# Local attention of a fused four-layer network: smaller pieces, one issue order read from a table, integer steps as two-operand instructions

## Chip, cores, metric

One NeuronCore of a Trainium2 chip runs the whole network as one launch. The metric is device time in microseconds (us) from start to end of the launch; lower is better. The core has five engines with queues of their own: PE (TensorE, matrix products; weight loads are listed as PEld), DVE (VectorE), ACT (ScalarE), POOL (GpSimd) and SP (which issues DMAs here). Each runs its instructions in the order of its queue and waits on semaphores for the others.

## What is computed

Four layers, each `x = x + attention(norm(x)) * silu(ffn(norm(x)))`, on x of 16 x 256 x 128 in fp32. The change lies in the feed-forward branch of the fourth layer, which is itself a small transformer of depth 2, and at its start in the end of the third layer (a mixture of experts, whose rows are gathered and weighted). Cut to what matters:

```python
def _layer(x, wqkv, qs, ksc, wo, lg, lb, w1, b1, w2, b2):     # DEPTH = 2 times
    h = shift_token(x)                        # second half of the columns moved by one token
    q, k, v = split(h @ wqkv)                 # 8 heads of 64
    q = l2norm(q) * qs ; k = l2norm(k) * ksc
    q, k = rotary_xpos(q, k)
    o = local_attention(q, k, v)              # windows of 64, each sees itself and the one before
    x = x + o @ wo
    h = shift_token(x)
    h = layernorm(h) * lg + lb
    a, g = split(h @ w1 + b1)
    return x + (a * gelu(g)) @ w2 + b2

# end of the third layer:
x = x + s * silu(sum over the 2 chosen experts of gate * (relu(x @ W1[e] + b1) @ W2[e] + b2[e]))
xn = layernorm(x)                             # input of the fourth layer
```

## The kernel before

`layer3` calls `local_attention` twice, with `gated_mlp` after each. I call the two calls the first and the second pass. Each works on 16 batches (b) of 256 tokens, which are two tiles (t) of 128 tokens on the partitions. For every batch it does, by the names of its inner functions (before, after in brackets where a letter is used):

- `begin`, `begun` (B, h; L1773, L1778, L1779, in the first pass also L1781): transpose the input tile on PE, copy it shifted into hT on ACT.
- `times` (T, V; L1785): one 128 x 512 projection on PE; j = 0 is q, 1 is k, 2 is v; twice each for the two tiles.
- `squares` (q; L1795): squares of q or k on ACT. `turned` (c, r; L1803 to L1812): their sums by head and the rotation, four instructions on DVE, and the sum `rot += sn` on POOL.
- `values` (v; L1818, L1821): copy of v on ACT, and a DMA from SP's queue that moves a half to other partitions.
- `lengths` (L, k; L1825, then `rsqrt` L1728 to L1738, and L1831): the inverse root of the lengths by an integer guess and three Newton steps, 13 instructions of 32 columns on DVE; then k is scaled on POOL, twice.
- `across` (X, x; L1838, L1841): q or k turned to have its columns on the partitions, PE then ACT.
- `scores` (S, m; L1849, L1858, L1867, L1869): for one half u of the heads, mask and 32 small products on PE into two PSUM banks (pool `ps`), then the negated maxima on DVE, times the lengths.
- `powers` (e; L1881): four exponentials of 128 x 128 on ACT with their sums; `shares` (d, p; L1894, L1895): reciprocal on DVE, scaling on POOL.
- `keys_first` (K, y; L1903, L1907): probabilities turned on PE, copied on ACT. `weigh` (W, o; L1916, L1926): 12 products with v on PE into the one bank of pool `po`, copied on ACT.
- `finish`, `finished` (F, A; L1932, L1941): output projection, and the sum into x on DVE.

The issue order is written out in a loop over i: the scores of batch i stand beside the projections of batch i+2, the turning of batch i+1 and the last half of batch i-1. `pin` ties every instruction to the one before it on its engine, so this order is each engine's order. PSUM has eight banks here: three rotate under the name `pm` (pt, pj, pr and pw, in order of allocation), two `ps`, two `pt`, one `po`. In SBUF, `sq` and `sn` have two buffers each, `rot` three, `p` and `pT` five.

In the first pass, `end(n)` from the third layer is called seven times ahead of the loop and twice in each round: it gathers two expert rows for tile n (L1508, an indirect DMA of POOL's queue, into three `got` buffers per name), weighs those of tile n-1 on DVE (L1518), and in a cycle of four takes one chunk of four tiles through the gated sum (Silu on ACT at L207, two products on DVE at L208, L209), the statistics (L896, L897, and a power on POOL, L158, L159) and the normalising (L904), which gives the next input tiles.

The function that makes the integer guess, before the change:

```python
nc.vector.tensor_scalar(guess, x.bitcast(I32), 1, None, ALU.logical_shift_right)              # L1728
nc.vector.tensor_scalar(guess, guess, -1.0, float(0x5F3759DF), ALU.mult, ALU.add)             # L1729
```

Of the kernel before, what the change touches and what calls it, by code (L numbers as in the profile page):

```python
# [72 lines left out]

class Net:
    def __init__(self, tc, ctx, a):
        self.tc, self.nc, self.a, self.ctx = tc, tc.nc, a, ctx
        nc = self.nc
        self.keep = ctx.enter_context(tc.tile_pool(name="keep", bufs=1))
        self.x = self.keep.tile([P, NT, D], F32, name="x")
        self.xn = self.keep.tile([P, NT, D], F32, name="xn")  # L80
        self.xnT = self.keep.tile([P, NT * P], F32, name="xnT")
        self.s = self.keep.tile([P, NT, D], F32, name="s")
        self.ident = self.const("ident")
        self.ones = self.keep.tile([P, P], F32, name="ones")
        nc.vector.memset(self.ones, 1.0)
        self.again = self.keep.tile([P, NT], F32, name="again")
        self.desc, self.before = self.const("desc"), self.const("before")
        self.mhalf = self.keep.tile([P, 32], F32, name="mhalf")
        nc.vector.memset(self.mhalf, -0.5)
# [741 lines left out]
    def layer2(self, ydram, consts, fin):  # L831
# [58 lines left out]
        at = {}  # L890

        def stats(c):
            mv = fin.tile([P, 4, 2], F32, name="ln_mv")
            for j in range(4):
                st = fin.tile([P, 6], F32, name="ln_st")
                nc.vector.bn_stats(st, self.x[:, 4 * c + j, :])  # L896
                nc.vector.bn_aggr(mv[:, j, :], st)  # L897
            at[c] = mv, self.rstd(fin, mv[:, :, 1], 4, EPS, "ln_r")

        def normed(c):  # L900
            mv, r = at.pop(c)
            for j in range(4):
                t = 4 * c + j
                nc.vector.tensor_scalar(  # L904
                    self.xn[:, t, :], self.x[:, t, :], mv[:, j, 0:1], r[:, j : j + 1], ALU.subtract, ALU.mult
                )

        def end(pool, n):


            if 0 <= n < NT:
                experts["bring"](pool, n)
            if 0 <= n - 1 < NT:
                experts["weigh"](n - 1)
            c, r = divmod(n - 5, 4)
            if 0 <= c < NT // 4 and r == 0:
                self.gated_add(fin, 4 * c, chunk(f, c), 4)
            if 0 <= c < NT // 4 and r == 1:
                stats(c)
            if 0 <= c < NT // 4 and r == 2:  # L920
                normed(c)

        return end
# [723 lines left out]
    def layer3(self, end, out):  # L1647
# [6 lines left out]
        with ExitStack() as ctx:  # L1654
            gp = ctx.enter_context(right("a3_g"))
            dram = ctx.enter_context(tc.tile_pool(name="a3_d", bufs=1, space=DRAM))
            for l in range(2):
                with right(f"f3_m{l}") as cp:
                    d = self.local_weights(cp, l)
                    mlp = self.mlp_weights(cp, l)  # L1660
                    if l == 0:
                        with tc.tile_pool(name="l2_g", bufs=3) as got:
                            self.local_attention(X, d, lambda n: end(got, n))
# [60 lines left out]
    def rsqrt(self, pool, x, n, name):  # L1724
# [3 lines left out]
        nc.vector.tensor_scalar(guess, x.bitcast(I32), 1, None, ALU.logical_shift_right)  # L1728
        nc.vector.tensor_scalar(guess, guess, -1.0, float(0x5F3759DF), ALU.mult, ALU.add)  # L1729
# [12 lines left out]
    def local_attention(self, X, d, end=None):  # L1742

# [7 lines left out]
        with ExitStack() as ctx:  # L1751
# [18 lines left out]
            def begin(b):  # L1770
# [4 lines left out]
            def begun(b):  # L1775
# [7 lines left out]
            def times(b, t, j):  # L1783
# [9 lines left out]
            def squares(b, t, j):  # L1793
# [3 lines left out]
            def turned(b, t, j):  # L1797
                if t == 0 and j == 0:
                    rows[b]["ss"] = vp.tile([P, 2, 2, 8], F32, name="ss")
                    rows[b]["rot"] = rp.tile([P, 2, 2, 512], F32, name="rot")  # L1800
                pj, sq = rows[b].pop(("pj", t, j)), rows[b].pop(("sq", t, j))
                rot = rows[b]["rot"][:, t, j, :]
                nc.vector.tensor_reduce(rows[b]["ss"][:, t, j, :], heads(sq), AX.X, ALU.add)  # L1803
                nc.vector.tensor_mul(heads(rot), heads(pj), wide(d["cos"][:, t, j, :]))
                sn = pool.tile([P, 512], F32, name="sn")
# [6 lines left out]
                nc.gpsimd.tensor_add(rot, rot, sn)  # L1812

            def values(b, t):
                if t == 0:
                    rows[b]["v"] = vv.tile([P, 3, 512], F32, name="v")
                v = rows[b]["v"]
# [5 lines left out]
            def lengths(b):  # L1823
                ss = rows[b]["ss"].rearrange("p t j h -> p (t j h)")
                nc.vector.tensor_scalar_max(ss, ss, 1e-24)  # L1825
                r = self.rsqrt(vp, ss, 32, "rl")
                rows[b]["r"] = r.rearrange("p (t j h) -> p t j h", t=2, j=2)
                for t in range(2):
                    k = heads(rows[b]["rot"][:, t, 1, :])
                    n = rows[b]["r"][:, t, 1, :].rearrange("p (h o) -> p h o", o=1)  # L1830
                    nc.gpsimd.tensor_mul(k, k, n.to_broadcast([P, 8, 64]))  # L1831

            def across(b, j):
                out = pool.tile([P, 4, S], F32, name="qk"[j] + "T")
                for t in range(2):
                    pr = psm.tile([P, 4, P], F32, name="pm")
                    for c in range(4):
                        nc.tensor.transpose(  # L1838
                            pr[:, c, :], rows[b]["rot"][:, t, j, c * P : (c + 1) * P], self.ident
                        )  # L1840
                    nc.scalar.copy(out[:, :, t * P : (t + 1) * P], pr)  # L1841
                rows[b]["qk"[j]] = out

            def scores(b, u):

                qT, kT, r = rows[b]["q"], rows[b]["k"], rows[b]["r"]
                ps = [psc.tile([P, 2, 2, P], F32, name="ps") for _ in range(2)]
# [4 lines left out]
                for c in range(2):  # L1852
                    for w, keys in enumerate(((0, 0), (64, 128))):
                        for half in range(2):
                            q0 = P * w + 64 * half
                            for i in range(2):
# [7 lines left out]
                                )  # L1864
                for i in range(2):
                    nm = vp.tile([P, 2, 2], F32, name="nm")
                    nc.vector.tensor_reduce(nm, ps[i], AX.X, ALU.max, negate=True)  # L1867
                    h = 4 * u + i
                    nc.vector.tensor_mul(  # L1869
                        nm, nm, r[:, :, 0, h : h + 3 : 2].rearrange("p w c -> p c w")  # L1870
                    )
                    rows[b]["ps", u, i] = ps[i], nm

            def powers(b, u, i):
                ps, nm = rows[b].pop(("ps", u, i))
# [3 lines left out]
                for c in range(2):  # L1879
                    for w in range(2):  # L1880
                        nc.scalar.activation(  # L1881
                            p[:, c, w, :],
                            ps[:, c, w, :],
                            AF.Exp,
                            scale=rows[b]["r"][:, w, 0, h + 2 * c : h + 2 * c + 1],
                            bias=nm[:, c, w : w + 1],
# [5 lines left out]
            def shares(b, u, i):  # L1892
                p, den = rows[b]["p", u, i], rows[b].pop(("den", u, i))
                nc.vector.reciprocal(den, den)  # L1894
# [4 lines left out]
            def keys_first(b, c):  # L1899
                pt = pst.tile([P, 2, 2, P], F32, name="pt")  # L1900
                for i in range(2):
                    for w in range(2):
                        nc.tensor.transpose(  # L1903
                            pt[:, i, w, :], rows[b]["p", c // 2, i][:, c % 2, w, :], self.ident
                        )
                rows[b]["pT", c] = pT = pp.tile([P, 2, 2, P], F32, name="pT")
                nc.scalar.copy(pT, pt)  # L1907

            def weigh(b, c):

                po = pso.tile([P, S], F32, name="po")
# [12 lines left out]
                if c == 0:  # L1924
                    rows[b]["o"] = pool.tile([P, 4, S], F32, name="oT")
                nc.scalar.copy(rows[b]["o"][:, c, :], po)  # L1926

            def finish(b):
                rows[b]["pw"] = pw = psm.tile([P, 2, D], F32, name="pm")
                for t in range(2):  # L1930
                    for c in range(4):
                        nc.tensor.matmul(  # L1932
                            pw[:, t, :],
                            rows[b]["o"][:, c, t * P : (t + 1) * P],
# [5 lines left out]
            def finished(b):  # L1940
# [3 lines left out]
            def run(f, b, *args):  # L1944
                if 0 <= b < B:
                    f(b, *args)

            mark = len(nc.cur_bb.bb.instructions)
            if end is not None:
                for n in range(7):  # L1950
                    end(n)
            for i in range(-3, B + 1):
                run(scores, i, 0)
                run(times, i + 2, 0, 0)
                run(squares, i + 2, 0, 0)
                run(powers, i, 0, 0)
                run(times, i + 2, 0, 1)
                run(squares, i + 2, 0, 1)
                run(turned, i + 2, 0, 0)
                run(keys_first, i - 1, 2)  # L1960
                run(powers, i, 0, 1)
                run(shares, i, 0, 0)
                run(turned, i + 2, 0, 1)
                run(keys_first, i - 1, 3)
                run(shares, i, 0, 1)
                run(across, i + 1, 0)
                run(weigh, i - 1, 2)
                run(times, i + 2, 0, 2)
                run(values, i + 2, 0)
                run(weigh, i - 1, 3)  # L1970
                if end is not None:
                    end(2 * i + 13)
                run(scores, i, 1)
                run(times, i + 2, 1, 0)
                run(squares, i + 2, 1, 0)
                run(powers, i, 1, 0)
                run(times, i + 2, 1, 1)
                run(turned, i + 2, 1, 0)
                run(squares, i + 2, 1, 1)
                run(finish, i - 1)  # L1980
                run(shares, i, 1, 0)
                run(finished, i - 1)
                run(powers, i, 1, 1)
                run(turned, i + 2, 1, 1)
                run(keys_first, i, 0)
# [116 lines left out]
```

## Time and profile before

| what | value |
|---|---|
| three runs (us) | 2974.58, 2992.75, 2987.36; median 2987.36 |
| the profiled execution | 2966.91, its span 2965.2 |
| busy in the span: PE, DVE, ACT, POOL | 2391.3 (81%), 1984.8 (67%), 1559.5 (53%), 1360.3 (46%) |
| first pass | 1548 to 1955 us of the span |
| second pass | 2087 to 2454 us |
| first pass: busy PE, DVE, ACT, POOL (1548 to 1965) | 329.4, 315.3, 285.8, 237.9 of 417 |
| second pass: the same (2084 to 2455) | 295.1, 254.9, 258.3, 179.0 of 371 |

The two passes are about a quarter of the span, and in neither is an engine busy throughout. A span is read best by stages: the shares of the whole mix stages with different limits. A line of the order of time gives start, length, engine, line, operation, what it writes and reads, how many instructions are merged in it, and in brackets how long the engine sat idle before it and what ended that.

### The profile page before, as it was taken

To read this page: it belongs to the slowest core of one execution; us is meant where nothing else is said; L and a number is where in the kernel's file an instruction comes from. 1 tells how busy PE (TensorE), PEld (TensorE's weight loads), DVE (VectorE), ACT (ScalarE), POOL (GpSimd) and SP (SyncE) were. 2 spreads that over 40 slices of the span, in tenths; PEclk is the share of its full clock that TensorE was granted. 3 is DMA by queue.
4 is the path that set the end of the run, shared out by engine and by line. 5 is a ranking of instruction groups with operands and counts; after the bars stand their busy time and mean duration, and the time that the engine had idled before them with its cause. 6 is when DMAs were issued, how large, how long until landed. Compare 5 with 4: busy or idle time off the path is not lost.

```text
span 2965.2 us, 47535 instructions
## 1 busy us (share of the span) xinstructions
PE 2391.3 (81%) x17543; PEld 1561.1 (53%) x17543; DVE 1984.8 (67%) x3841; ACT 1559.5 (53%) x3490; POOL 1360.3 (46%) x1084
## 2 busy tenths in 40 slices
PE   5999983669856589998967787868788878789988
PEld 3666662556532355555544555555355555555555
DVE  4666523335479788888869888624677744488885
ACT  1555561213344466666636777721577763456564
POOL 2000002113236666666666665432455533299896
PEclk8999986779967899999987999978999999899898
DMA  2111002000013455555540000000100000111110
GB/s 64 27 26 30 12 4 98 4 15 13 16 59 123 145 172 188 180 175 187 187 141 26 22 25 17 12 1 0 45 14 14 14 8 4 39 38 45 31 48 8
DMA packets 136915, 168.88 MB, mean 57 GB/s; under 512 B 20850, under 2 KB 100988, under 8 KB 136684
## 3 DMA queue, kind: packets, MB, share of 16 engines
q1 hardware_dynamic: 128108, 147.75, 17.1%
q0 software_dynamic: 6496, 17.05, 1.7%
q8 instruction: 139, 2.28, 0.3%
q10 hardware_dynamic: 2080, 1.05, 0.1%
q14 instruction: 92, 0.75, 0.1%
HBM read 127.62 MB, written 29.79 MB: 53 GB/s over the span
## 4 chain that ended last, share of the span: by engine, by line
PE 24%; DVE 15%; ACT 14%; POOL 8%; issue 3%; DMA 3%; SPq 1%; POOLq 0%; DVEq 0%; ACTq 0%
ACT p L1881 6%; PE py L1192 3%; POOL e L313 3%; DVE nm L1867 2%; PE ps L1858 2%; PE ph L2035 2%; ACT pT L1907 1%; PE po L1916 1%; PE ph L1435 1%; PE pa L1037 1%; PE ph L2039 1%; PE pa L325 1%; PE py L2051 1%; DMA xr<-f_x 1%; PE pb L335 1%
## 5 line engine op out<-in xcount | busy, mean ns | idle before, releaser
L346 DVE TENSOR_REDUCE nmax<-pa 128x2 f32<-128x512 f32 x512 | 329.8, 685 | 137.1 <-PE pb L335 109.5
L356 ACT ACTIVATE e<-pb 128x512 f32<-128x512 f32 x512 | 286.2, 594 | 228.1 <-PE pb L335 199.8
L335 PE MATMUL pb<-qa,kT 32*128 32x256 f32 x2048 | 385.4, 422 | 25.5 <-ACT e L356 25.5
L325 PE MATMUL pa<-kT,qT 32*128 32x256 f32 x2048 | 364.8, 434 | 19.0 <-DMA kT<-qkd 17.5
L1182 POOL TENSOR_TENSOR hc<-st,cn 128x1024 f32<-128x1024 f32 x111 | 261.2, 2353 | 194.6 <-DVE dbb L1165 117.1
L1169 DVE TENSOR_TENSOR_SCAN st<-dab,dbb 128x1024 f32<-128x1024 f32 x128 | 292.7, 2287 | 24.5 <-ACT dab L1155 9.1
L325 PEld LDWEIGHTS pa<-kT,qT 32*128 32x128 f32 x2048 | 231.5, 200 | 100.9 <-issue 53.5
L335 PEld LDWEIGHTS pb<-qa,kT 32*128 32x128 f32 x2048 | 248.7, 195 | 54.6 <-ACT e L356 46.4
L1192 PE MATMUL py<-hc,ident 128*128 128x512 f32 x512 | 267.7, 613 | 10.3 <-DVE hc L1182 8.7
L1812 POOL TENSOR_TENSOR rot<-rot,sn 128x512 f32<-128x512 f32 x128 | 163.2, 1276 | 225.1 <-DVE den L1894 162.1
L313 POOL TENSOR_TENSOR e<-e,pen 128x1024 f32<-128x1024 f32 x96 | 228.5, 2390 | 57.8 <-ACT e L356 57.1
L1881 ACT ACTIVATE p<-ps,nm,rl 128x128 f32<-128x128 f32 x512 | 229.0, 474 | 28.6 <-DVE nm L1869 18.7
L1785 PE MATMUL pm<-wqkv,hT 128*128 128x512 f32 x384 | 210.1, 661 | 41.7 <-DVE sn L1807 28.9
L1155 ACT ACTIVATE dab<-dl,A_log 128x512 f32<-128x512 f32 x256 | 177.8, 719 | 103.7 <-DVE st L1169 57.5
L158 POOL TENSOR_SCALAR ln_r<-ln_mv 128x4 f32<-128x4 f32 x32 | 7.4, 233 | 465.9 <-DVE ln_st L168 419.1
L1165 DVE TENSOR_TENSOR dbb<-du,bn 128x1024 f32<-128x1024 f32 x128 | 188.8, 1475 | 5.0 <-DMA bn<-dr 2.4
L1867 DVE TENSOR_REDUCE nm<-ps 128x4 f32<-128x512 f32 x128 | 87.6, 684 | 107.8 <-PE ps L1858 106.5
L1895 POOL TENSOR_TENSOR p<-p,den 128x512 f32<-128x512 f32 x128 | 133.6, 1044 | 52.9 <-DVE den L1894 45.5
L1795 ACT ACTIVATE sq<-pm 128x512 f32<-128x512 f32 x128 | 77.1, 602 | 145.2 <-PE pm L1785 140.1
L1916 PE MATMUL po<-pT,v 128*64 128x64 f32 (+1 forms) x1536 | 95.3, 265 | 64.2 <-ACT oT L1926 49.6
L1192 PEld LDWEIGHTS py<-hc,ident 128*128 128x128 f32 x512 | 91.7, 195 | 81.2 <-issue 61.8
L1916 PEld LDWEIGHTS po<-pT,v 128*64 128x64 f32 x1536 | 76.5, 150 | 109.6 <-ACT oT L1926 83.0
(382 smaller groups left out, 5582.0 us busy)
## 6 DMA issues: line engine op xcount, KB each, us to landing
bn<-dr SPq DMA_DIRECT2D x64, 512.0 KB
cn<-dr SPq DMA_DIRECT2D x64, 512.0 KB
w<-in_L_ffn_W_dram SPq DMA_DIRECT2D x94, 256.0 KB
qkd<-qk SPq DMA_DIRECT2D x32, 256.0 KB
v<-v SPq DMA_DIRECT2D x64, 128.0 KB
f_y<-y SPq DMA_DIRECT2D x47, 128.0 KB
f_x<-zero POOLq DMA_DIRECT2D x8, 704.0 KB, 8.3
xr<-f_x SPq DMA_DIRECT2D x44, 128.0 KB
```

Source lines behind the costliest of these rows:

```text
L313: eng.tensor_mul(pairs[m], pairs[m], pen.to_broadcast([P, 2, 2, S]))
L325: nc.tensor.matmul(pa[:, t, :], qbuf[b % 4][r : r + 32, g, ts], kbuf[b % 4][r : r + 32, g, :], start=True, stop=True,)
L335: nc.tensor.matmul(pb[:, t, :], kbuf[b % 4][r : r + 32, g, ts], qas[m // 8][r : r + 32, g % 2, :], start=True, stop=True,)
L346: nc.vector.tensor_reduce(nbuf[n // 8 % 2][:, :, u // 4, u % 4, 8], pa, AX.X, ALU.max, negate=True)
L356: nc.scalar.activation(e, pb, AF.Exp, scale=scale)
L1165: mul = nc.vector.tensor_mul(db, du, d["bn", n])
L1169: nc.vector.tensor_tensor_scan(wide(d["st", r]), wide(d.pop(("da", r))), wide(db), 0.0, ALU.mult, ALU.add)
L1182: ins = eng.tensor_mul(d["hc", r], d.pop(("st", r)), d["cn", r // 4 * 2])
L1192: nc.tensor.matmul(d["py", h], self.ident, d["hc", r - r % 2][:, r % 2, :], start=(n == 0), stop=(n == N - 1))
L1785: nc.tensor.matmul(pj, hTs[b % 3][:, t * P : (t + 1) * P], d["qkv"][:, j * 512 : (j + 1) * 512], start=True, stop=True,)
L1881: nc.scalar.activation(p[:, c, w, :], ps[:, c, w, :], AF.Exp, scale=rows[b]["r"][:, w, 0, h + 2 * c : h + 2 * c + 1], bias=nm[:, c, w : w ...
L1916: nc.tensor.matmul(po[64 * i : 64 * i + 64, P * w + q0 : P * w + q0 + n], v[:, k, hs], pT[:, i, w, q0 : q0 + n], start=True, stop=True, ti ...
```

## The change

- The inner functions of `local_attention` are cut so that each piece belongs to one engine: a copy out of PSUM is no longer issued by the function that made the product, the rotation's POOL sum is a piece of its own (r), and so are the reciprocal (d), the maxima (m) and the two scalings of k (k).
- The pieces are issued in the order of a table, `LOCAL` for the second pass and `LOCAL_END` for the first. An entry `e01:0` is the piece e with arguments 0, 1 for batch i + 0. The rows reach from -2 to 3, so that the loop makes one round more than before.
- In `LOCAL`, turning of q (X00, X01) stands ahead of the second scores (S1), which follow both exponentials of the first half; the output projection (F) and its sum (A) belong to batch i-2. In `LOCAL_END`, the scores and maxima of batch i+1 close the round, and the first projection of batch i+3 (T00) is in it too.
- `m` multiplies the maxima of both banks by the lengths in one instruction of eight columns, where there were two of four.
- The third layer's end becomes pieces as well: `Ga`, `Gb` gather, `wa`, `wb` weigh one tile and then take the first chunk that has something to do one step further (normalising, statistics or sum), `su` is Silu, `pw` the power on POOL. `B` calls `need`, which weighs on until its tiles are normalised. `got` has four buffers.
- The two integer steps take their constants from a tile `ints` (set by two POOL memsets at the start) as second operand.

```diff
+LOCAL = """
+    F:-2 y1:-1 S0:0 W0:-1 T00:2 m0:0 o0:-1 p10:-1 q00:2 e00:0 A:-2 W1:-1 e01:0 X00:1 c00:2 K2:-1 o1:-1
+    r11:1 T01:2 d01:0 q01:2 y2:-1 K3:-1 V0:2 x00:1 d00:0 y3:-1 S1:0 W2:-1 X01:1 k1:1 c01:2 p01:0 o2:-1
+    T10:2 x01:1 W3:-1 m1:0 v0:2 q10:2 o3:-1 V1:2 T11:2 r00:2 v1:2 c10:2 p00:0 k0:1 q11:2 r01:2 K0:0
+    X10:1 e10:0 x10:1 c11:2 X11:1 r10:2 x11:1 e11:0 B:3 L:2 K1:0 d10:0 y0:0 d11:0 h:3 p11:0
+"""
+
+LOCAL_END = """
+    T01:2 p10:-1 W1:-1 p11:-1 q00:2 q01:2 r11:1 K2:-1 c00:2 X00:1 V0:2 c01:2 K3:-1 o1:-1 y2:-1 W2:-1
+    e00:0 e01:0 X01:1 S1:0 Gb:1 pw:2 o2:-1 y3:-1 W3:-1 d00:0 x00:1 k1:1 p00:0 wa:0 r00:2 v0:2 d01:0 k0:1
+    x01:1 r01:2 p01:0 o3:-1 T10:2 wb:0 q10:2 T11:2 m1:0 c10:2 K0:0 q11:2 K1:0 e10:0 Ga:0 e11:0 V1:2 F:-1
+    c11:2 v1:2 X10:1 A:-1 r10:2 d11:0 y0:0 X11:1 x10:1 x11:1 B:3 su:-1 W0:0 h:3 S0:1 d10:0 L:2 o0:0
+    T00:3 y1:0 m0:1
+"""
...
+        self.ints = self.keep.tile([P, 2, 32], I32, name="ints")
+        nc.gpsimd.memset(self.ints[:, 0, :], 1)
+        nc.gpsimd.memset(self.ints[:, 1, :], 0x5F3759DF)
...
+        def silu():
+            c = len(gates)
+            if n["weighed"] >= 4 * (c + 1):
+                gates[c] = fin.tile([P, 4, D], F32, name="gate")
+                nc.scalar.activation(gates[c], chunk(f, c), AF.Silu)
...
+        def power():
+            c = n["power"]
+            if c in mvs:
+                rs[c] = self.rstd(fin, mvs[c][:, :, 1], 4, EPS, "ln_r")
+                n["power"] = c + 1
+
+        def weigh():
+            if n["weighed"] < n["got"]:
+                experts["weigh"](n["weighed"])
+                n["weighed"] += 1
+            any(step(c) for c in range(n["normed"], NT // 4))
...
-                        with tc.tile_pool(name="l2_g", bufs=3) as got:
-                            self.local_attention(X, d, lambda n: end(got, n))
+                        with tc.tile_pool(name="l2_g", bufs=4) as got:
...
+                            self.local_attention(X, d, end)
...
-        nc.vector.tensor_scalar(guess, x.bitcast(I32), 1, None, ALU.logical_shift_right)
-        nc.vector.tensor_scalar(guess, guess, -1.0, float(0x5F3759DF), ALU.mult, ALU.add)
+        nc.vector.tensor_tensor(guess, x.bitcast(I32), self.ints[:, 0, :n], ALU.logical_shift_right)
+        nc.vector.tensor_tensor(guess, self.ints[:, 1, :n], guess, ALU.subtract)
...
+            @piece
+            def r(b, t, j):
+                rot = rows[b]["rot"][:, t, j, :]
+                nc.gpsimd.tensor_add(rot, rot, rows[b].pop(("sn", t, j)))
...
+            @piece
+            def k(b, t):
+                k = heads(rows[b]["rot"][:, t, 1, :])
+                n = rows[b]["r"][:, t, 1, :].rearrange("p (h o) -> p h o", o=1)
+                nc.gpsimd.tensor_mul(k, k, n.to_broadcast([P, 8, 64]))
...
+            @piece
+            def m(b, u):
+
+                rows[b]["nm", u] = nm = vp.tile([P, 2, 2, 2], F32, name="nm")
                 for i in range(2):
-                    nm = vp.tile([P, 2, 2], F32, name="nm")
-                    nc.vector.tensor_reduce(nm, ps[i], AX.X, ALU.max, negate=True)
-                    h = 4 * u + i
-                    nc.vector.tensor_mul(
-                        nm, nm, r[:, :, 0, h : h + 3 : 2].rearrange("p w c -> p c w")
-                    )
...
+                    nc.vector.tensor_reduce(nm[:, i], rows[b]["ps", u][i], AX.X, ALU.max, negate=True)
+                n = rows[b]["r"][:, :, 0, 4 * u : 4 * u + 4].rearrange("p w (c i) -> p i c w", i=2)
+                nc.vector.tensor_mul(nm, nm, n)
...
-                for n in range(7):
-                    end(n)
-            for i in range(-3, B + 1):
-                run(scores, i, 0)
...
+                for n in "Ga Ga wa Ga wa Ga wa wa su Ga wa Ga wa pw Ga Ga wa".split():
+                    end[n]()
+            order = []
+            for n in (LOCAL if end is None else LOCAL_END).split():
...
+            late = max(row for *_, row in order)
+            for i in range(-late, B + 2):
+                for n, args, row in order:
+                    b = i + row
+                    if n in ("Ga", "Gb", "wa", "wb", "su", "pw"):
+                        end[n]()
+                    elif 0 <= b < B:
+                        do.get(n[0] + "_", do.get(n[0]))(b, *args)
```

## Prediction

> **What bounds the kernel now.** I read, in this order: the chain of waits of the page, the busy time by stretches, the waits of the second local attention, and the order of time of one batch in it. The page's chain says first where to look:
>
> ```profile
> ACT p L1881 6%; PE py L1192 3%; POOL e L313 3%; DVE nm L1867 2%; PE ps L1858 2%; PE ph L2035 2%; ACT pT L1907 1%; PE po L1916 1%; PE ph L1435 1%; PE pa L1037 1%; PE ph L2039 1%; PE pa L325 1%; PE py L2051 1%; DMA xr<-f_x 1%; PE pb L335 1%
> ```
>
> Its largest line is the exponential of the small attention, and five of the first eight lie in that function. No line holds a stage alone: the chain hops between engines. The stretches (columns: length; busy us of PE, weight loads, DVE, ACT, POOL; granted clock; DMA share; GB/s) give two batches of the first pass and six of the second:
>
> ```profile
> 1682.42:1730.18 47.76, 38.34 (x357) 25.09 (x357) 41.10 (x107) 36.09 (x111) 31.64 (x31) 0.93 0.09 23
> 2146.94:2272.22 125.28, 105.18 (x1073) 70.15 (x1075) 95.29 (x252) 95.43 (x312) 66.51 (x60) 1.00 0.06 14
> ```
>
> So a batch costs 23.88 us in the first pass while expert rows are still gathered (47.76/2) and 20.88 in the second (125.28/6), and no engine is full: in the second PE is busy 17.5, DVE 15.9, ACT 15.9, POOL 11.1 per batch. Where the rest goes, by the waits of 2084 to 2455 (us, times, longest):
>
> ```profile
> DVE nm L1867 <- PE ps L1858: 73.9, 31, 5.6
> ACT sq L1795 <- PE pm L1785: 73.6, 36, 5.5
> ```
>
> About 2.3 us each, twice a batch. The order of time shows one of them on ACT and what PE does meanwhile:
>
> ```profile
> 2209.09 0.37 ACT L1926 COPY oT<-po 128x256 f32<-128x256 f32 x1 [0.28 <-PE po L1916]
> 2211.71 0.60 ACT L1795 ACTIVATE sq<-pm 128x512 f32<-128x512 f32 x1 [2.25 <-PE pm L1785]
> ...
> 2208.37 0.67 PE L1916 MATMUL po<-pT,v 128*64 128x128 f32 x12 [0.86 <-ACT oT L1926]
> 2208.98 0.60 PE L1849 MATMUL ps<-maskb,identb 128*128 128x512 bf16 x2
> 2209.51 1.10 PE L1858 MATMUL ps<-kT,qT 64*64 64x128 f32 x32
> 2210.55 1.99 PE L1785 MATMUL pm<-wqkv,hT 128*128 128x512 f32 x4
> ```
>
> PE waits for ACT's last copy of oT, then does the scores and one projection; ACT has nothing until that projection ends. Twice a batch the two stand in line behind each other: 2 x 2.25 plus scraps is the gap from 15.9 to 20.88. Last, two 32-element steps on DVE and what POOL does then:
>
> ```profile
> 2216.82 1.20 DVE L1728 TENSOR_SCALAR rl_i<-ss 128x32 int32<-128x32 int32 x1
> 2218.05 0.96 DVE L1729 TENSOR_SCALAR rl_i<-rl_i 128x32 int32<-128x32 int32 x1
> ...
> 2216.71 1.27 POOL L1812 TENSOR_TENSOR rot<-rot,sn 128x512 f32<-128x512 f32 x1
> 2217.93 1.05 POOL L1895 TENSOR_TENSOR p<-p,den 128x512 f32<-128x512 f32 x1
> ```
>
> Each ends when POOL's instruction ends; the second took 0.18 in the fill of the passes, where POOL is idle.
>
> **What the Trainium skill says.** "SBUF — State Buffer", section "SBUF: two separate sides": VectorE and GpSimd share one port pair as an exclusive lock, which a DVE instruction in a two-port mode, or with two SBUF inputs while GpSimd reads SBUF, has to wait for. The trace agrees for both kinds: the lines above, and L1869, with two SBUF inputs, takes 0.16 when POOL is idle and 0.57 beside a k scaling. So the new two-operand integer steps are not free of that lock. "ScalarE: Activation LUTs", section "What ACT_TABLE_LOAD costs": 1283 ns a load; the trace has 1283. "TensorE: Matmul & The Clock Gate", section "What's actually happening": the clock gate opens with activity; here the 32 score products take 1.10 at full clock and 1.99 after PE has stood.
>
> **The change, part by part.** The amount of arithmetic stays: the same matmuls, exponentials, copies and rotations, 64 gathers, 8 gated sums. Pitches in us, start to start in the second pass: PE: T (one projection) 0.91, S 1.57, W 0.60, X and K 0.45, F 1.78, B 0.3; ACT: q 0.49, e (four exponentials) 1.75, y 0.46, x and v 0.48, o 0.27, h 0.8; DVE: c 1.86, m 1.5, L 2.65 without the lock (13 steps of about 0.2), d 0.17, A 0.35; POOL: r 1.24, k 1.02, p 1.04. Sums of a batch: PE 16.7, ACT 15.6, DVE 14.1, POOL 11.2. None can go below 16.7.
>
> *Second pass, steady round (LOCAL).* I lay the pieces by hand in table order, from E, the end of e11, taking 0.1 to 0.25 from one engine to the next. PE had B, K1 and F in front, so S0 runs E+0.1 to 1.75, beside ACT's y0, h, y1 (1.7). Then W0, T00: o0 ends at 2.75, q00 at 4.05; ACT loses 1.5 here. m0 (1.75 to 3.3) meets POOL's r11 with its two-SBUF product and ends near 3.9: still covered. e00, e01 to 7.55; o1, q01, y2, x00, y3 to 9.7: this is the block that now covers S1, whose scores wait for e01. o2, x01, v0 to 11.4; q10 (behind T10, which needs the bank of c01) 12.0; o3, v1 13.5; q11 14.4 (ACT loses 1.6 from 9.7 on). m1 is done at 12.3, so e10, x10, x11, e11 run on to 18.85. B waits for c11 (16.4), then B, K1, F reach 19.0. Round: **19.1**, against 20.88. L lies after r10 and before d10, d11, so POOL waits and the lock costs it nothing; the new waits on the two sn buffers (c01 for r11, c10 for r00, c11 for r01) are met by 1 to 4 us.
>
> From the first to the 15th batch's scores: 14 x 1.8 = 25. Fill: two L of 3.6 become 2.6: 2. The last but one round, 20.8 before with PE cooling (scores 1.84), has no projections: S 1.6 + m 1.6 + e 3.5 twice and two copies, near 16: 4. Tail: one S ahead of other work and the merged m, against p11 now in front of p10 on POOL and K2 behind it: 3 by the sum of the pieces (23 against 24.6), cut to 2. Second pass: **33 to 34** less.
>
> *First pass (LOCAL_END).* ACT: 15.6, plus the xnT copy 0.4 and per two batches one Silu 0.5 with two table loads 2.57: 17.5; the loads are still there. DVE is nearest to full: 41.10 of 47.76 in two batches. The integer steps lose 1.20 + 0.96 - 0.4 = 1.8 a batch. But in this table d10 stands right in front of L, so p10, p11 and r11 run on POOL (3.4 us) just then, and the first steps of L wait for them one by one; after them come two gathers, during which DVE goes free. I take L = 5.7, that is 3.0 of lock. DVE per batch: 20.55 - 1.8 + 3.0 = 21.75, with 0.75 of idle 22.5: 1.4 less than 23.88. Bounds of the lock: 0 (then DVE needs 18.8 and ACT with its stalls sets about 20: 3.9 less) to all 13 steps behind POOL (below). Some 10 batches with gathers x 1.4 = 14; four later ones, near 21 before, at about 19.5: 6; fill and drain as above: 5. First pass: **25** less. The extra got buffer and the prologue in the order gather, weigh, Silu change the start by no more than 1: before, the first sum already came right after its Silu, which waited for the gathers; POOL's pow still stands behind two gathers. `need` should find the tiles normalised two rounds ahead.
>
> *At nothing:* two POOL memsets of 32 columns at the start (hidden by the load of x; 0.3 if not); SP's queue has the same DMAs in the same order (v's half copies, two a batch, are read by W a round later).
>
> Sum: 34 + 25 = 59. The profiled execution took 2966.91 (span 2965.2); that gives 2908. The median shown is 2987.36, 20 above it, so I forecast **2928**.
>
> **Rivals.**
> 1. *The lock is mild in the first pass* (DVE finds gaps, L near 2.8): 3.9 x 10 instead of 14, and the steady rounds at 18.5: 25 + 8 more, 2895. For it: POOL is idle a third of the time. Chance 0.2.
> 2. *The first pass gains nothing*: DVE's longer list (weigh, gate, statistics now between c01 and m1) pushes m1, and e10 and e11 behind it. Only the second pass is left: 34, 2953; with half of that too, 2970. For it: DVE at 86% busy there. Chance 0.2.
> 3. *Slower: L is caught by POOL step by step.* If POOL keeps reading SBUF through all of L, its 13 steps take about 1.04 each, 13.5 against my 5.7: 7.8 more in 13 batches is 101, so 42 slower, 3029. It decides from L about 10.2 on, where 4.5 x 13 has eaten the 59. Against it: gathers and a short pow follow r11. Chance 0.07.
> 4. *The table does not take hold*: a pm bank or sn buffer turns the order back into the old line-up: 2987. Against it: every engine's order in the built program is the table's. Chance 0.05.
>
> **How the numbers follow.** Forecast 0.48 (2910 to 2945), rivals 0.2, 0.2, 0.07, 0.05. 1% is 30 us, about what runs of this kernel can tell. Faster by over 1%: 0.48 + 0.2 + 0.13 of rival 2 = 0.81; within: 0.12; slower: 0.07. The range runs from 2885 (rival 1) to 2965 (most of rival 2).
>
> **What would show it.** Second pass: scores every 19.1 us, one ACT stall of about 1.5 behind the score products in place of two of 2.25, L1728's successor at 0.2. First pass: rounds of 22.5, DVE over 90% busy, the same integer step long (about 1) beside p10. It is wrong if the rounds of the second pass stay above 20, if those of the first exceed 24, or if the square still waits twice a batch for its projection.

## The result, and the profile after

The changed kernel takes **2940.48 us** (median of 4 runs, 2938.90 to 2941.29) beside 2985.76 for the kernel before (4 runs, 2974.58 to 2992.75). The ratio is 0.9851, with a 95% interval of 0.982 to 0.9882, so 45 us less by the medians. The profiled executions show less of it: spans of 2965.2 before and 2939.2 after, 26 apart, because the profiled execution of before lay below all its timed runs, and that of after at its median.

The time of the kernel before goes with the mean granted clock of its runs. Of its 49 runs that the comparisons below list with a clock, the nine under 0.890 have a median of 2990.95, the ten at 0.897 or more (all of one comparison) 2969.15. The four runs of the changed kernel have 0.897 to 0.901. At a like clock I therefore estimate the change at some 29 us (2969.15 less 2940.48), close to the 26 of the traces; the rest of the 45 goes with a lower clock of the runs of before. Which of the two follows from the other, no run tells. In the trace I compare stages, not totals.

The page's chain of waits, after. The exponential of the small attention, 6% and first before, is at 4%, and the maxima, the scores, the copies pT and the products po are no longer in the list; the projections (L1851) and F (L2024) of that function are:

```profile
PE py L1238 4%; ACT p L1961 4%; POOL e L333 3%; PE pm L1851 2%; PE pm L2024 2%; PE ph L1481 2%; PE ph L2090 2%; PE pa L345 1%; PE pa L1083 1%; PE ph L2094 1%; PE py L1504 1%; PE py L2106 1%; PE pb L355 1%; DMA xr<-f_x 1%; DVE pen L1670 1%
```

The stretches, after: ten batches of the first pass with their gathers, then six of the second (length; busy us of PE, weight loads, DVE, ACT, POOL; granted clock; DMA share; GB/s):

```profile
1588.10:1830.50 242.40, 183.43 (x1706) 121.83 (x1716) 229.15 (x509) 181.32 (x538) 156.59 (x145) 0.94 0.09 22
2153.00:2267.70 114.70, 104.00 (x1064) 69.81 (x1072) 86.38 (x241) 98.18 (x312) 66.66 (x61) 1.00 0.07 15
```

A batch of the second pass costs 114.70/6 = 19.1 us, 20.9 before. A batch of the first costs 24.2, and the same stretch of ten took 237.9 before, 23.8 each: the rounds with gathers have not become shorter, although DVE is now busy 95% of them.

In the waits of 2065 to 2430 (us, times, longest) what is left of the two leading stalls of the second pass, each 73 to 74 us before, is this:

```profile
ACT sq L1866 <- PE pm L1851: 30.6, 49, 5.4
DVE nm L1950 <- PE ps L1937: 25.3, 17, 1.6
```

The order of time in a round of the second pass, after, on DVE and on POOL: L runs while POOL has nothing, and its integer steps take 0.19 where they took 1.20 and 0.96.

```profile
2263.28 0.17 DVE L1899 TENSOR_SCALAR ss<-ss 128x32 f32<-128x32 f32 x1
2263.49 0.19 DVE L1777 TENSOR_TENSOR rl_i<-ss,ints 128x32 int32<-128x32 int32 x1
2263.71 0.19 DVE L1778 TENSOR_TENSOR rl_i<-ints,rl_i 128x32 int32<-128x32 int32 x1
...
2260.93 1.27 POOL L1886 TENSOR_TENSOR rot<-rot,sn 128x512 f32<-128x512 f32 x1 [0.74 <-DVE sn L1877]
2266.24 2.04 POOL L1980 TENSOR_TENSOR p<-p,den 128x512 f32<-128x512 f32 x2 [4.04 <-DVE den L1975]
```

POOL's last rotation ends at 2262.20 and its next product begins at 2266.24. All 13 steps of L lie in that gap.

In the first pass it is the other way round. First one group of before (ten batches), then the same group and its neighbours after (busy, mean ns | idle before):

```profile
L904 DVE TENSOR_SCALAR xn<-x,ln_mv,ln_r 128x128 f32<-128x128 f32 x20 | 9.1, 516 | 0.0
```

```profile
L931 DVE TENSOR_SCALAR xn<-x,ln_mv,ln_r 128x128 f32<-128x128 f32 x20 | 18.9, 1003 | 0.0
L943 DVE TENSOR_TENSOR gate<-gate,s 128x512 f32<-128x512 f32 x5 | 8.8, 1754 | 0.0
L944 DVE TENSOR_TENSOR x<-x,gate 128x512 f32<-128x512 f32 x5 | 7.1, 1416 | 0.2
L1961 ACT ACTIVATE p<-ps,nm,rl 128x128 f32<-128x128 f32 x160 | 70.8, 463 | 26.5 <-DVE nm L1952 26.4
```

The normalising took twice as long, the gate's product 1754 ns against 693, and the exponentials waited 26.4 us for the maxima, which these steps had pushed back, against 3.8 before. The table has put these steps beside r00, k0, r01 and p01 on POOL.

### The profile page after: what moved, and what is told of

Its sections match the earlier page's. It is cut to its first block, busy times and chain, and to the rows that moved or that the text cites. A ratio compares the mean times of both kernels' runs of the same rounds, so it can differ in the third digit from the quotient of the medians.

```text
span 2939.2 us, 47407 instructions
## 1 busy us (share of the span) xinstructions
PE 2381.4 (81%) x17515; PEld 1559.3 (53%) x17543; DVE 1989.5 (68%) x3777; ACT 1571.4 (53%) x3488; POOL 1369.1 (47%) x1086
## 4 chain that ended last, share of the span: by engine, by line
PE 27%; DVE 16%; ACT 8%; POOL 8%; issue 3%; DMA 3%; SPq 1%; POOLq 0%; DVEq 0%; ACTq 0%
PE py L1238 4%; ACT p L1961 4%; POOL e L333 3%; PE pm L1851 2%; PE pm L2024 2%; PE ph L1481 2%; PE ph L2090 2%; PE pa L345 1%; PE pa L1083 1%; PE ph L2094 1%; PE py L1504 1%; PE py L2106 1%; PE pb L355 1%; DMA xr<-f_x 1%; DVE pen L1670 1%
## 5 line engine op out<-in xcount | busy, mean ns | idle before, releaser
L355 PE MATMUL pb<-qa,kT 32*128 32x256 f32 x2048 | 386.7, 422 | 26.1 <-ACT e L376 26.0
L1851 PE MATMUL pm<-wqkv,hT 128*128 128x512 f32 x384 | 206.8, 644 | 53.5 <-ACT p L1961 21.0
L1504 PEld LDWEIGHTS py<-w,h 128*128 128x128 f32 x752 | 100.8, 196 | 61.2 <-issue 39.5
L402 PE MATMUL pm<-e,vaug 128*32 128x256 f32 x2048 | 128.2, 392 | 3.1 <-DVE s L436 3.1
L1851 PEld LDWEIGHTS pm<-wqkv,hT 128*128 128x128 f32 x384 | 64.0, 195 | 102.4 <-issue 39.2
```

What stands on the lines that cost most here:

```text
L355: nc.tensor.matmul(pb[:, t, :], kbuf[b % 4][r : r + 32, g, ts], qas[m // 8][r : r + 32, g % 2, :], start=True, stop=True,)
L1851: nc.tensor.matmul(pj, hTs[b % 3][:, t * P : (t + 1) * P], d["qkv"][:, j * 512 : (j + 1) * 512], start=True, stop=True,)
```

## The stages, run by run

All of this table is worked out from the traces: the starts of the maxima (the first in a batch), of the first gather, and of the first maxima of the third attention. The last row's kernel is the fastest one found.

| kernel | first gather to first maxima | ten rounds with gathers | five rounds after them | second pass, 14 rounds | second pass, first maxima to third attention |
|---|---|---|---|---|---|
| before | 57.6 | 237.9 | 110.1 | 292.4 | 452.1 |
| first pass as before | 57.6 | 243.5 | 108.5 | 267.0 | 421.5 |
| second pass as before | 63.0 | 245.1 | 100.1 | 293.3 | 452.1 |
| integer steps as before | 63.5 | 244.5 | 98.5 | 266.9 | 421.7 |
| changed | 63.2 | 242.4 | 98.1 | 265.9 | 423.4 |
| weighing moved | 62.5 | 239.6 | 102.4 | 266.9 | 421.4 |
| weighing and prologue moved | 60.8 | 239.8 | 101.4 | 266.9 | 422.1 |
| L ahead | 63.2 | 238.5 | 93.8 | 266.1 | 420.5 |
| L ahead, both moved | 60.3 | 232.3 | 95.5 | 266.0 | 420.3 |

Read down the columns: a stage is the same to about 3 us wherever its table is the same, but for the rounds with gathers, which scatter by some 5 us. The stage of ten rounds runs slightly past its last gather, and the fifth of the rounds after it has no projections left to do.

## The experiments

**One pass at a time.** The function of before is kept beside the new one, and called for one pass (for the first pass together with the third layer's end of before).

```
-                            self.local_attention(X, d, end)
+                            self.local_attention_old(X, d, lambda n: end(got, n))   # first pass as before
...
-                        self.local_attention(X, d)
+                        self.local_attention_old(X, d)                              # second pass as before
```

> The first pass in its order from before (gathers and third layer's end too), the second by the new table, two-operand integer steps in both. Theory (the first pass gains next to nothing, because DVE waits more on the port shared with POOL): its rounds return to 23.9 us, its stretch to about 407, the whole within 10 of the changed kernel, 2940 to 2950. Rival (the first pass brought a good part of the gain, as I forecast with 25): 2960 to 2970.

Measured: 2953.69, ratio 0.9931 (0.9904 to 0.9958), between the two ranges.

> The first pass by the new table, the second in its order from before. Theory: the gain of about 27 in the second pass is lost, 2965 to 2980, and the rounds of the second pass return to 20.9. Rival (the gain sits in the first pass): 2945 to 2955.

Measured: 2967.83, ratio 0.9981 (0.997 to 0.9992), in the range of the theory: the gain sits in the second pass. The kernel before stood at 2973.19 beside these two, 10 to 15 lower than in the other comparisons, so the share of a pass is a range: the second is worth 20 (against before) to 30 (2967.83 less the 2937.51 of the next run), the first 5 to 16. In the trace the first pass shows, from the first gather to the first maxima of the second, 590.6 before, 597.4 in the run with the old first pass, and 591.3 after.

**The integer steps alone.** The changed kernel with the two lines of before in the inverse root (the tile `ints` and its memsets go too).

```
-        nc.vector.tensor_tensor(guess, x.bitcast(I32), self.ints[:, 0, :n], ALU.logical_shift_right)
-        nc.vector.tensor_tensor(guess, self.ints[:, 1, :n], guess, ALU.subtract)
+        nc.vector.tensor_scalar(guess, x.bitcast(I32), 1, None, ALU.logical_shift_right)
+        nc.vector.tensor_scalar(guess, guess, -1.0, float(0x5F3759DF), ALU.mult, ALU.add)
```

> The changed kernel with the integer steps of before (one operand and constants). Theory (the port lock meets both forms alike, and the tables decide when POOL is busy): within 5 of 2940, the two steps as long as with two operands. Rival (two operands avoid the lock): 1.5 to 2 us a batch in the first pass, 2960 or more.

Measured: 2937.51, ratio 0.987 (0.9834 to 0.9906). The new form brings nothing. The old one takes 0.18 where POOL is idle, the new one 0.19, and 0.93 each beside p10: the place decides, not the form. The second step in a round of the first pass, in the new form (changed kernel) and in the old one (this run):

```profile
1706.28 0.93 DVE L1778 TENSOR_TENSOR rl_i<-ints,rl_i 128x32 int32<-128x32 int32 x1
...
1713.06 0.93 DVE L1775 TENSOR_SCALAR rl_i<-rl_i 128x32 int32<-128x32 int32 x1
```

**The lock on L in the second pass.** The table of the second pass with the order that the first has: the reciprocals d11 and d10, for which POOL's scalings p11 and p10 wait, ahead of L. Then the same with the scaling k0, which needs L, put ahead of p11 and p10 in POOL's row, so that POOL stands still during L.

```
-    ... B:3 L:2 K1:0 d10:0 y0:0 d11:0 h:3 p11:0
+    ... B:3 d11:0 d10:0 L:2 K1:0 y0:0 h:3 p11:0            # the first run
+    ... B:3 d11:0 d10:0 L:2 k0:2 K1:0 y0:0 h:3 p11:0       # the second; k0:1 taken out further up
```

> The new table of the second pass with both reciprocals ahead of the inverse root, so that two scalings of probabilities run on POOL beside its 13 steps. Theory (a lock costs only where DVE is the engine that is full): those steps take 4.5 to 5 us a batch in place of 2.7, the round of the second pass stays within 0.5 of 19.1, the whole within 8 of 2940. Rival (any lock on these steps reaches the end): 2 us a batch, 2970.

Measured: 2994.98, ratio 1.0076 (1.0053 to 1.0099): 55 us more than the changed kernel, so the theory that a later L would be covered fell, and the loss is more than the rival's 2 us a batch as well. The 14 rounds took 314.5, 22.5 each.

> The second pass with d11 and d10 ahead of L, as in the run that was 55 us slower, but with the scaling k0 of the batch whose lengths L gives put in front of p10 in GpSimd's row, so that GpSimd has to wait for L's end and L meets no lock. Theory (of the 3.3 us that a round became longer there, 2.7 were L's lock, 5.3 instead of 2.65, and the rest that L waits for the last exponential): L takes about 2.7, rounds near 20 to 20.5, 2953 to 2966. Rival (the wait for the exponential is what costs, or GpSimd's late p10): rounds of 22 and over, 2985 or more.

Measured: 2952.75, ratio 0.9901 (0.987 to 0.9932), at the low end of the theory, 14 rounds in 284.0, 20.3 each. The order of time on DVE and on POOL, in the first of the two kernels:

```profile
2246.35 0.15 DVE L1899 TENSOR_SCALAR ss<-ss 128x32 f32<-128x32 f32 x1
2246.54 1.06 DVE L1777 TENSOR_TENSOR rl_i<-ss,ints 128x32 int32<-128x32 int32 x1
2247.64 0.96 DVE L1778 TENSOR_TENSOR rl_i<-ints,rl_i 128x32 int32<-128x32 int32 x1
2248.52 1.29 DVE L1780 TENSOR_SCALAR rl_h<-ss 128x32 f32<-128x32 f32 x1
...
2251.63 1.28 DVE L1950 TENSOR_REDUCE nm<-ps 128x4 f32<-128x512 f32 x2
...
2246.52 2.04 POOL L1980 TENSOR_TENSOR p<-p,den 128x512 f32<-128x512 f32 x2 [3.91 <-DVE ss L1899]
2248.51 1.26 POOL L1886 TENSOR_TENSOR rot<-rot,sn 128x512 f32<-128x512 f32 x1
```

and in the second:

```profile
2257.06 0.15 DVE L1899 TENSOR_SCALAR ss<-ss 128x32 f32<-128x32 f32 x1
2257.24 0.19 DVE L1777 TENSOR_TENSOR rl_i<-ss,ints 128x32 int32<-128x32 int32 x1
...
2259.61 1.28 DVE L1950 TENSOR_REDUCE nm<-ps 128x4 f32<-128x512 f32 x2
...
2259.84 1.04 POOL L1907 TENSOR_TENSOR rot<-rot,rl 128x512 f32<-128x512 f32 x1 [6.45 <-DVE rl L1787]
```

From L's start to the maxima it is 5.28 us with the lock and 2.55 without. So of the 3.4 us that a round had become longer, 22.5 - 20.3 = 2.2 went with the lock; I put the other 1.2 down to L's wait for the last exponential. The split takes it that k0's new place costs or gains nothing by itself, which was not tried. In L itself the instructions are the same: only what POOL does at that moment differs. That is what the Trainium skill, "SBUF — State Buffer", section "SBUF: two separate sides", says of the port pair, and here three steps of L were caught, one behind each of POOL's two products p and its rotation, and the other ten were not, since POOL's next instruction, the scaling of k, waits for L's end.

**The order of the turns.** In the second pass X00 and x00 put behind S1, where the products of q and k stood before the change.

```
-    ... e01:0 X00:1 c00:2 ... V0:2 x00:1 d00:0 y3:-1 S1:0 W2:-1 X01:1 ...
+    ... e01:0 c00:2 ... V0:2 d00:0 y3:-1 S1:0 X00:1 x00:1 W2:-1 X01:1 ...
```

> The changed kernel with the first turning of q in the second pass behind the second scores instead of in front of them. Theory (that turning and its copy are part of what covers the scores): 0.3 to 1 us a batch, 5 to 16 over 2940. Rival (the cover is long enough without it): no difference.

Measured: 2948.47, ratio 0.9883 (0.9856 to 0.9909), 14 rounds of 272.3, 19.45 each: in the range of the theory. Some 8 us of the second pass's gain hang on this one piece and its copy.

**What holds the rounds with gathers.** First the weighing moved to where POOL reads less: wa to the start of the round, wb behind m1. Then the prologue alone, with the seventh gather ahead of the power, and both.

```
-    T01:2 p10:-1 ... p00:0 wa:0 r00:2 ... T10:2 wb:0 q10:2 T11:2 m1:0 c10:2 ...
+    wa:0 T01:2 p10:-1 ... p00:0 r00:2 ... T10:2 q10:2 T11:2 m1:0 wb:0 c10:2 ...
...
-    "... su Ga wa Ga wa pw Ga Ga wa"
+    "... su Ga wa Ga wa Ga pw Ga wa"
```

> The changed kernel with the third layer's steps at two other places of the first table: the first weighing opens the round, ahead of the rotations (POOL gathers or waits then), the second follows the second maxima (POOL gathers). Theory (the new cost of the first pass is the port lock on weighing, sum and normalising): sum and normalising fall from about 3.2 and 3.8 us to 1.4 and 1.1 to 2, two rounds from 49.5 to about 45, the whole 15 to 30 less than 2940. Rival (the length of DVE's list ahead of the second maxima decides, or the table loads): as long a round or longer, 2935 to 2950.

Measured: 2939.33, ratio 0.9853 (0.9825 to 0.9881). The stretch of ten rounds and the groups of this kernel:

```profile
1590.10:1829.70 239.60, 181.53 (x1706) 120.67 (x1716) 194.61 (x509) 182.73 (x539) 151.13 (x145) 0.93 0.09 22
```

```profile
L1961 ACT ACTIVATE p<-ps,nm,rl 128x128 f32<-128x128 f32 x160 | 70.7, 466 | 1.5 <-DVE nm L1952 1.5
L931 DVE TENSOR_SCALAR xn<-x,ln_mv,ln_r 128x128 f32<-128x128 f32 x20 | 6.4, 400 | 0.0
L943 DVE TENSOR_TENSOR gate<-gate,s 128x512 f32<-128x512 f32 x5 | 3.4, 683 | 0.0
```

The move did what it was meant to do: DVE is busy 194.61 instead of 229.15, and the exponentials wait 1.5 instead of 26.4. But 34.5 us less of busy time gave 2.8 us of length, which the five rounds behind took back (98.1 to 102.4), and nothing measurable of the whole: the 15 to 30 of the theory did not come. **DVE at 95% was not the only bound:** with it at 81% something else held the rounds at nearly the same length.

> The changed kernel with the seventh tile's gathers ahead of the power on POOL in the prologue, as they stood before. Theory: the first input tile is turned 3 to 4 us earlier, the whole 2 to 4 less than 2940. Rival (the fill waits for something else): no difference.

Measured: 2938.49, ratio 0.9843 (0.9821 to 0.9864). The start is 1.9 shorter in the trace (63.2 to 61.3); the whole is 2.0 shorter, no more than its runs scatter.

> Both together. Theory: the two gains add up, 18 to 34 less than 2940, and faster than the kernel before by about 65. Rival: as 2940.

Measured: 2936.14, ratio 0.9839 (0.9818 to 0.986), 4 us under the changed kernel where the theory had 18 to 34. With DVE less busy, two of the waits between 1610 and 1805 in this kernel suggest what the rounds follow:

```profile
DVE nm L1950 <- PE ps L1937: 29.6, 8, 5.1
...
PE pm L1851 <- DVE sn L1877: 26.3, 8, 3.8
```

Each waits for the other: the maxima for the scores, and a projection (which stands ahead of those scores on PE) for the bank that a rotation on DVE empties. I read them as a loop: L, m0, c00 and c01, projection, turns, S1, m1, c10 and c11, then L of the next round. L with its lock would be a link of it. So I moved L ahead of d10 and d11 in the first table, once on the changed kernel and once on the one with both moves.

```
-    ... r10:2 d11:0 y0:0 X11:1 x10:1 x11:1 B:3 su:-1 W0:0 h:3 S0:1 d10:0 L:2 o0:0
+    ... r10:2 y0:0 X11:1 x10:1 x11:1 B:3 su:-1 W0:0 h:3 S0:1 L:2 d10:0 d11:0 o0:0
```

> The changed kernel with one thing moved in the table of the first pass: the inverse lengths L stand ahead of the two reciprocals d10 and d11, as they do in the table of the second pass, so that GpSimd has to wait for L's end with p10, p11 and r11. Theory (L's lock is part of the loop that sets the rounds with gathers: L, m0, the rotations c00 and c01, the projection that waits for their bank, the scores S1, m1, c10, c11, L): L falls from about 5.1 us to about 2.7, and the rounds from about 24.5 to 22.5; over the 12 rounds with gathers 18 to 28 us less than the changed kernel, 2912 to 2923. Rival (VectorE's other work, which is locked elsewhere, fills the round, and the lock moves to the steps that now lie beside p10, p11 and r11): within 6 us of 2940. Another rival (GpSimd, held back by 3 us, delays the gathers and the products p behind them): slower by 5 to 15.

Measured: 2927.98, ratio 0.9818 (0.9772 to 0.9864).

> The same move of L on top of the two moves of before (weighing of gathered rows moved within the round, and the prologue's gather ahead of its power). With them VectorE is no longer full in the first pass (195 us busy of 240 in ten rounds against 229), and yet the rounds stayed at 24: the theory says that they follow the loop through L. So here the lock of L should count in full: 20 to 30 us less than the 2936 of the two moves without it, 2906 to 2916. Rival (the rounds are held by ScalarE's table loads and the matmul order): within 6 us of 2936.

Measured: **2926.34**, ratio 0.9794 (0.9755 to 0.9833), the fastest of the kernels that compute the whole result. These are 12 and 10 us less than the kernels that they start from, where the theory had 18 to 28 and 20 to 30, and the rival at most 6: L is a link of what holds the rounds, but only a part of its lock came through. One round of the second kernel on DVE:

```profile
1698.47 0.19 DVE L1777 TENSOR_TENSOR rl_i<-ss,ints 128x32 int32<-128x32 int32 x1
1698.70 0.19 DVE L1778 TENSOR_TENSOR rl_i<-ints,rl_i 128x32 int32<-128x32 int32 x1
...
1701.49 1.29 DVE L1950 TENSOR_REDUCE nm<-ps 128x4 f32<-128x512 f32 x2 [0.41 <-PE ps L1937]
```

L's lock is gone (2.6 us in place of 5.2), and of the 2.5 a round about 0.75 came through in the ten rounds with gathers (239.8 to 232.3) and 1.2 in the five after them (101.4 to 95.5). From the fifth on the rounds now alternate, 22.1 and 25.6. Those with 25.6 hold the gate's Silu with its two table loads, and on DVE the gate's product, the sum and the statistics. The last run tells these two apart: a plain copy stands in for the Silu, so its nonlinearity is left out of the result.

```
-                nc.scalar.activation(gates[c], chunk(f, c), AF.Silu)
+                nc.scalar.copy(gates[c], chunk(f, c))
```

> The kernel with L ahead and the two moves (2926), with a plain copy in place of the Silu of the gate, so that the gate's nonlinearity is left out and ScalarE loads no tables in the first pass: 12 loads of 1.28 us fall away, 15.4 in all, 2.57 in every second round. There the rounds are 25.6 long against 22.1 in between. Theory (the loads lie on the loop: the one ahead of the copies of h delays the square, the one behind it the exponentials of the same round): the long rounds fall to 23 to 23.8, 12 to 16 us less, 2910 to 2914. Rival (the long rounds are set by VectorE, which puts the second weighing and the statistics ahead of c10 and c11, for whose banks TensorE waits 2.3 us): they stay above 25, within 5 us of 2926.

Measured: 2922.62, ratio 0.9783 (0.9748 to 0.9818); the long rounds that were 25.6 stay at 25.1 to 25.7. Taking away twelve loads of 1.28 gave 4 us, not 15, and no more than the runs scatter (2918.72 to 2929.96): the rival held. The waits of 1605 to 1795 in this kernel are the same loop:

```profile
DVE nm L1950 <- PE ps L1937: 28.0, 9, 5.2
...
PE pm L1851 <- DVE sn L1877: 22.6, 8, 3.6
```

What stays open: that the gate's steps on DVE ahead of the rotations c10 and c11 make the long rounds long fits these waits, but moving them behind those rotations was not tried.

## Why the prediction was right, and where it was not

The forecast of 2928 missed 2940.48 by 12, inside its range. The sum of 59 was 45 by the medians, but 26 in the traces, nearly all of it in the second pass: the number came closer than the account behind it. Step by step:

- **Second pass, steady rounds: right, mechanism and size.** Forecast 19.1, measured 19.1; 14 rounds gave 292.4 - 265.9 = 26.5 against 25 (3.4 of it in the first round, which pays back the fill below; the other 13 gave 1.8 each). L met no lock, and the stalls shrank: the square still waits for its projection, three times a batch now, which by its letter is one of the prediction's signs of being wrong, but for 0.6 us each (30.6 in 49 waits) instead of 2.0 (73.6 in 36). The two counter-experiments, L behind d11 and X00 behind S1, show that both parts carry it: 3.4 and 0.45 us a round. What F and A one batch later and the merged maxima add was not tried apart.
- **Last but one round and tail: 4 + 2 forecast, 2 measured in this pair of traces, about 5 in the others.** The round went from 21.3 to 15.6, as forecast, but from the last maxima to the third attention the changed kernel took 142.0 against 138.4. The two trade: in the eight runs that share this second pass, the round took 15.5 to 18.0, and both together 154.2 to 155.3, against 159.7 before.
- **Second pass, fill: wrong in sign.** The two shorter L were to bring 2. From the first projection to the first maxima it was 26.1 before and 30.4 after, 4.2 more; the short first round (17.6 for 21.0) gives 3.4 of that back. Neither L became shorter: they took 3.73 and 3.74, before 3.72, since one integer step took 1.27 beside a rotation on POOL. In the run with k0 ahead of p11 both took 2.66, and the fill 27.7. The rest I read from the order of time on PE; no run changed it. In the changed kernel:

```profile
2102.98 0.81 PE L1913 MATMUL pm<-ident,rot 128*128 128x128 f32 x4 [2.19 <-DVE sn L1877]
2104.47 5.49 PE L1851 MATMUL pm<-wqkv,hT 128*128 128x512 f32 x6 [0.68 <-ACT qT L1920]
```

  and as many projections in the fill of before:

```profile
2107.70 2.99 PE L1785 MATMUL pm<-wqkv,hT 128*128 128x512 f32 x6 [0.67 <-ACT v L1818]
```

  In the table's order a turn stands ahead of the projections of the next part. In the steady round its input is long there; in the fill PE waits 2.19 for it, and the projections behind it come late and take 5.49 for three, against 2.99.
- **First pass: the step that failed** is "DVE per batch: 20.55 - 1.8 + 3.0 = 21.75, with 0.75 of idle 22.5: 1.4 less than 23.88", and with it "10 batches with gathers x 1.4 = 14". The prediction calls itself wrong if these rounds exceed 24, and they do: 24.2 here, 24.05 to 24.5 in the other runs with this table. L itself was sized well: 5.7 forecast, 5.15 measured (1705.88 to 1711.03). Three things were not. The 20.55 was carried over as if the rest of DVE's list kept its durations; it rose, and DVE was busy 22.9 a batch. DVE's idle time was put at 0.75 without a reason and was 1.3. And DVE's busy time was taken for the only bound: with it down to 19.5 the rounds were still 24.0. The ten rounds gave nothing: 242.4 against 237.9, or 243.5 in the run with the old first pass.
- **First pass, later rounds: a gain as forecast, though not at the level forecast.** The five rounds took 98.1 against 110.1 and 108.5. The first four went from 22.5 each (21.8 in the run with the old first pass) to 20.7, so 4.5 to 7.2 less in all, where 6 was forecast, but from 21 to 19.5. The last, without projections, went from 20.2 to 15.4, which I had booked under the drain. **The start** was to move by no more than 1 and became 5.6 longer (57.6 to 63.2). The prediction has POOL's power "behind two gathers"; the prologue has it ahead of the seventh tile's gathers, and that explains 2. The rest stays open. With it the whole first pass, from its first gather to the second pass's first maxima, gained nothing in this pair of traces (590.6 to 591.3), and 6 beside the run with the old first pass.
- **The two-operand steps: right that they are not free of the lock.** The 1.8 a batch credited to them in the first pass was 1.0: 1.20 + 0.96 before (means over the ten batches), 0.19 + 0.93 after, and 0.18 + 0.93 in the run with the old form. It comes from L's new place.
- **Rivals.** By the traces it is rival 2 that came true: the first pass gained nothing, and the second alone is left. It also saw the maxima pushed and the exponentials behind them (waits up to 4.4), though taking that away did not shorten the rounds. Rival 1's price was not to be had: with L free of its lock in the first pass, 12 to 14 us followed, not 33. Rival 3 did not come: POOL's gathers and power follow its rotation, as argued, and L stayed at half of the 10.2 from which it decides. But its mechanism is real: at 2.2 us a round, against the 7.8 it was priced at, it is the larger part of what made the run with L behind d11 the only one slower than before.
- **The offset, and luck.** I added 20 us for a profiled execution that ran below its median; the one of after ran at its median. From one profiled execution to the other the forecast was 2908, and 2940.99 came, 32 off. That the number landed within 12 is in part luck: the offset made up for most of the gain that the first pass did not bring.

## What to carry to other kernels

An engine at 95% busy need not be the only bound: take its busy time away and see whether the stage follows. If it does not, look for two engines that each wait for the other, since such a loop can set the round. Place short VectorE steps that share the port with GpSimd where GpSimd has to wait for their result, and then check what else has moved beside it. Cost the fill and the start of a hand-ordered table by themselves, since the order that fitted the steady round made PE wait there.

## What was not expected of the hardware

- The lock is paid in whole instructions of GpSimd, whatever the size of VectorE's own: a step on 128x32 goes from 0.19 to 0.93 to 1.29, the gate's product on 128x512 from 0.69 to 1.75, and GpSimd loses too (in the changed kernel, at 1693.36, a scaling of k took 1.49 where 1.04 is usual, and the rotation behind it 1.72 for 1.27).
- In the fastest kernel the 16 matmuls of F took 2.02 us after waits of up to 1.8, and 3.18 to 3.37 after waits of 2.33, in three of the long rounds. The length of the wait does not settle it: in the changed kernel waits of 3.34 were followed by 3.53, 2.64, 3.60 and 2.02.
- The median of the kernel before went from 2973.19 to 2987.99 from one comparison to the next, with the median of its listed clocks going from 0.896 to 0.890. The kernels with the new first pass had medians of 0.898 to 0.903 in all of them, but for the run with L behind d11 (0.894), and the run with the old first pass had 0.894. Why these stand at a lower clock stays open.
